# Transposing token rows and score maxima as 64-row products instead of full-array ones in a transformer block on one core

## Chip, core and metric

The kernel runs on one core of one Trainium2 chip. The metric is the device time of one execution in microseconds (us). Before the change it was 718.34 us, the median of three runs (718.19, 718.34 and 720.58). About 0.5%, 3.6 us, is what a measurement of this kernel can tell from no change.

## What is computed

A PixArt block over 16 sequences of 256 tokens and 256 channels: self-attention on a modulated layer norm, cross-attention to a context of 256 tokens, and an MLP of width 1024. Attention has 16 heads of 16 channels.

```python
x_norm = modulate(_ln(x), shift_a, scale_a)
q, k, v = split(x_norm @ W_qkv + b_qkv)                 # 16 heads of 16
x = x + gate_a * (softmax(q k^T * hd**-0.5) v @ W_proj + b_proj)
q_c = _ln(x) @ W_qc + b_qc
k_c, v_c = split(_ln(context) @ W_kvc + b_kvc)
x = x + softmax(q_c k_c^T * hd**-0.5) v_c @ W_cproj + b_cproj
h = gelu(modulate(_ln(x), shift_m, scale_m) @ W_mlp1 + b_mlp1)
x = x + gate_m * (h @ W_mlp2 + b_mlp2)
```

## The kernel before

**Units and beats.** There are 32 attention units: a self unit ("s") and a cross unit ("c") for each of the 16 sequences. The order is five s units, then s and c by turns, and c units at the end. The main loop (`for n in range(-1, nu)`, L1268) gives every unit eight beats, `beat(n, k)` with k from 0 to 7 (L1103). In a beat the tensor engine works on several units at once: raw scores of unit n+1 for its row maxima (`s_tile`, L697, PSUM tile `s`), transposed scores of unit n (`t_part`, L741, PSUM tile `st`), values of unit n or n-1, and projections of units n+2, n+3 and n-2. PE, ScalarE (ACT) and the other engines each issue in the order in which the code is written, so what stands first in `beat` runs first on its engine.

**The pieces of a beat on PE.** `visit` (L1079) issues four products into `s` and four into `st`; between the two it can call `between()`. Behind them `exps` lets ACT read the whole tile `st` through the exponential into a tile `pt`. `st` has one buffer, so nothing can be written into it until that exponential has read it. In the odd beats 24 projection products follow, in the even beats 16 value products (`av_part`, L771), written `o<-pt,v` in the profile. These use 32 columns of the array each and are float32.

**Lanes.** Projections have 64 rows: `lane` (L451) yields the 12 products of one projection on one half of the rows, and `lanes` (L471) pairs two of them, one on rows 0 to 63 and one on rows 64 to 127. A pair runs side by side; it is called a step below. `s` and `st` products (63 and 64 rows) run in such pairs too. `run` (L478) issues a number of steps.

**Transpositions.** A source (normed tokens `xn`, 2 x 128 tokens by 256 channels) is turned by four full-array products against `ident` into a PSUM tile `psT` (`turn` in `transposed`, L377). ACT then rounds it into the high part `xTh`, and DVE or GpSimd makes the rest, `xTl`. Each unit's source T[0] is turned in beat 0 (two products) and beat 2 (two) of the unit three before it; the second source of a c unit, T[1], is turned in beat 4 (four). The row maxima `mx` that DVE takes from `s` are turned by one product for half a unit's heads (`m_turn`, L728), in beat 0 and beat 4. ACT negates the result into `m` (`m_row`, L735), and a transfer writes it into row 63 of the query stack. The product of the maxima goes to a short-lived PSUM tile `psm`, into `psT` (beat 0, with a source) or into `st` (beat 4, with T[1]).

**PSUM.** `ps_gen` (L67) hands out three buffers of the tag "tr" (SHORT: `psT`, `psm`, `o`, q and k projections) and one of the tag "gen" (LONG: v and output projections).

Of the kernel before, what the change touches and what calls it, by code (L numbers as in the profile page):

```python
# [16 lines left out]
P = 128  # L17
# [4 lines left out]
def pixart_block(  # L22
# [29 lines left out]
                return tc.keep_in_program_order(i) if self.on else i  # L52
            return issue

    E_ = {'M': ((-46, -37, -26, -24, -20, -20, -18), (-26, -17, -10, -8, 1, 1, 1), (-3, 1, 4, 7, 9, 9, 9), (8, 11, 13, 15)), 'LN': {'s': 'pool', 'c': 'pool', 'q': 'pool'}, 'ON': (1, 1, 1), 'H': (7, 11, 14, 15), 'AP': 23, 'DV': (1, 2), 'E': (-14, -6, -2, 2), 'HP': (1, 0, 2), 'W1P': [(-9, 3), (-8, 3), (-7, 3), (-6, 3), (-4, 5), (-4, 7), (-3, 1), (-3, 5)], 'W2P': [(-4, 3), (-4, 7), (-3, 2), (-3, 4), (-3, 6), (-3, 7), (-2, 0), (-2, 2), (-2, 4), (-2, 6), (-1, 0)], 'PRE': 'z0qp z0kp load ld2 ld3 rest L0a L0b silu b9 brow turn b2 L0f scale hik lok T0t shift b1 T0h T0l hiq one0a loq hiv bk K0a K0m L1a L1n lov L2a L2b bq K0h K0x K0y L1e K0l K0s Q0a Q0m Q0h Q0x0 Q0y0a T1t Q0l Q0s0 Q0r ldm T1h V0a V0b z1qa T1l bv L2c z1kp L3a L3b L3p L3c K1a K1b', 'SL': {(-1, 0): 'Q1a Q1b K1x K1y K1l K1s', (-1, 1): 'T2t T2h T2p V1a Q1x Q1y Q1l Q1s', (-1, 2): 'V1b rest', (-1, 3): 'rest z2ka', (-1, 4): 'M0 rest one1 ld4', (-1, 5): 'K2a vone', (-1, 6): 'K2m z2qa', (-1, 7): 'cpm2 c1 one2', (0, 0): 'cpm0 rest', (0, 1): 'rest', (0, 4): 'rest', (1, 0): 'rest', (1, 2): 'rest', (1, 4): 'rest'}}
# [321 lines left out]
    def transposed(src, name, scale=None, pool=False):  # L377

        o = Box()

        def place():
            o.ps = ps_gen(f"psT_{name}", SHORT)

        def turn(fs=range(KC)):
            if len(fs) == KC:
                place()
            for f in fs:
                for t in range(NT):
                    PE.transpose(o.ps[:, f * N + t * P:f * N + (t + 1) * P],
                                 src()[:, t, f * P:(f + 1) * P], ident)  # L390

        def high():
# [78 lines left out]
    def lanes(x, y):  # L471


        if x:
            x.ps, x.fresh = ps_gen(f"ps_{x.name}", LONG if x.tok else SHORT), True
        return zip_longest(*(lane(o, half) for half, o in enumerate((x, y)) if o))

    def run(steps, n=12):  # L478
        for _ in islice(steps, n):
# [248 lines left out]
    def m_turn(u, hf, pst=None):  # L728
# [3 lines left out]
        PE.transpose(pst[:16, :P], u.mx[:, hf].rearrange("p r a t -> p (r a t)"), ident)  # L732
        return pst

    def m_row(u, hf, pst):  # L735

        m = work.tile([16, P], F32R, tag="m", name=f"m_{u.n}_{hf}", bufs=1)
        ACT.mul(m, pst[:16, :P], -1.0)
        SP.dma_start(u.q[63:P:64, 4 * hf:4 * hf + 4, :].bitcast(F32), m.bitcast(F32))

    def t_part(u, pair, par):  # L741
# [26 lines left out]
            for f in pieces:  # L768
                next(f)

    def av_part(u, g):  # L771
# [8 lines left out]
        if g == 3:  # L780
            o_out(u, 1)

    def o_out(u, half):
# [295 lines left out]
    def visit(n, k, home=sp, between=None):  # L1079
# [13 lines left out]
        in_turn(*t)  # L1093
        later.append(lambda: exp(units[n], k))

    def spare(n, gate=True):
        p1, _, p3 = (v and v.post for v in map(unit, (n - 1, n - 2, n - 3)))
        if p3 and not p3.added:
# [4 lines left out]
    def beat(n, k):  # L1103
# [25 lines left out]
        kp = None  # L1129
        if k == 5 and lx and n:  # L1130
            kp = lanes(q3.K, None if alone else p2)
        visit(n, k, between=kp and (lambda: run(kp, 2)))
        if k == 0:
            exps()
            if prev:
                av_part(prev, 3)
            if q3 and q3.ready:
                q3.T[0].place()
                pst = m_turn(cur, 1, q3.T[0].ps[:, N:])
                q3.T[0].turn((0,))  # L1140
            else:
                pst = m_turn(cur, 1)
            if prev:
                p1.pull_sums(1)
            m_row(cur, 1, pst)
            if q2:
                q2.K.low()
                q2.K.send_low()
# [3 lines left out]
                p2.low()  # L1152
        elif k == 1:
            exps()
            run(lanes(q2 and q2.Q, q2 and n and q2.V))
            if prev:
                p1.pull_values(1)
            if lc:
# [6 lines left out]
        elif k == 2:  # L1165
            exps()
            if cur:
                av_part(cur, 0)
            if q3:
                q3.T[0].turn((1,) if q3.ready else (0, 1))  # L1170
            if ls:
                ls.ln[0].steps[0]()
            elif prev:
# [24 lines left out]
        elif k == 4:  # L1198
# [2 lines left out]
                p2.end()  # L1201
            if cur:
                av_part(cur, 1)
            if lx:
                lx.T[1].turn()
            if nxt:
                m_part(nxt, 0, st[:, 0] if lx else None)
            if q2:
                q2.Q.low()
                q2.Q.send_low()  # L1210
# [7 lines left out]
                ls.ready = True  # L1218
        elif k == 5:
            exps()  # L1220
            run(kp or lanes(q3 and q3.K, (None if alone else p2) if n else q2.V))
            if cur:
                o_out(cur, 0)
            if lc:
# [8 lines left out]
        elif k == 6:  # L1233
# [139 lines left out]
```

## Time and profile before

| what | number |
|---|---|
| median of three runs | 718.34 us |
| the profiled execution, first to last instruction | 719.7 us |
| granted TensorE clock, mean | 0.999 |
| stage 45 to 490 us (attention): PE busy | 443.51 of 445.00 us |
| the same stage: DVE, ACT, POOL busy | 380.12, 369.82, 335.86 us |
| stage 540 to 719 us (MLP): PE busy | 174.71 of 179.00 us |

A timeline row gives the start in us, the length in us, the engine, operation, output<-inputs, and how many instructions were merged into the row. Product rows overlap, because the recorded length of one product (0.27 to 0.28 us) holds its way through the array; what a product costs is read from one start to the next.

### The profile page before, as it was taken

The page shows a single profiled execution, that of the slowest core. Times are in us where ns is not written, and L with a number is a line of the kernel's source. Part 1 is how long each engine was busy: PE and PEld are TensorE (multiplying, and loading weights), DVE is VectorE, ACT ScalarE, POOL GpSimd, SP SyncE. Part 2 cuts the span into 40 slices and gives each one's busy share as a digit, 9 for nine tenths or more (in the row PEclk, how much of TensorE's full clock was granted, in tenths as well). Part 3 has the DMA queues.
Part 4 walks back from the last instruction along what each step waited for, and adds up shares of the span by engine and source line. Part 5 has one row for each costly group of instructions (what it writes and reads, how often), then busy time and mean ns, then how long its engine had stood idle before and what let it go on. Part 6 is the DMA issues. An engine that isn't in the chain of part 4 may idle for free.

```text
span 719.7 us, 22488 instructions
## 1 busy us (share of the span) xinstructions
PE 710.4 (99%) x8993; PEld 592.3 (82%) x8993; DVE 567.8 (79%) x895; ACT 551.7 (77%) x955; POOL 520.6 (72%) x518
## 2 busy tenths in 40 slices
PE   9999999999999999999999999999999999999997
PEld 8777777777877778777787777777779999999997
DVE  5878888888888798888888888888675777777653
ACT  5677888888888788887888888887867677666661
POOL 7655778787776867776686798977857988656651
PEclk9999999999999999999999999999999999999999
DMA  7574455554545456454655656456323132313212
GB/s 236 183 233 157 160 170 178 175 179 160 167 151 196 162 176 191 163 166 153 195 167 176 210 174 195 156 192 196 95 78 103 59 87 61 88 46 88 66 39 74
DMA packets 81548, 106.15 MB, mean 147 GB/s; under 512 B 16610, under 2 KB 44548, under 8 KB 81444
## 3 DMA queue, kind: packets, MB, share of 16 engines
q1 hardware_dynamic: 80548, 104.37, 45.5%
q8 instruction: 71, 1.16, 0.7%
q10 hardware_dynamic: 896, 0.35, 0.2%
q14 instruction: 33, 0.27, 0.1%
HBM read 35.89 MB, written 8.98 MB: 62 GB/s over the span
## 4 chain that ended last, share of the span: by engine, by line
PE 94%; DVE 3%; POOL 2%; issue 0%; ACT 0%; POOLq 0%; ACTq 0%
PE s L51 18%; PE o L51 16%; PE st L51 16%; PE ph L51 12%; PE ps_qc L51 4%; PE ps_kc L51 4%; PE ps_k L51 4%; PE ps_q L51 3%; PE ps_v_c L51 3%; PE ps_v_s L51 3%; PE ps_P_s L51 2%; DVE mx L51 2%; PE ps_P_c L51 2%; PE psT_c L51 2%; PE psT_s L51 2%; PE psT_q L51 1%
## 5 line engine op out<-in xcount | busy, mean ns | idle before, releaser
L51 DVE TENSOR_REDUCE mx<-s 128x4 f32<-128x1024 f32 x252 | 307.9, 1222 | 73.5 <-PE s L51 70.1
L51 ACT ACTIVATE pt<-st 128x1024 f32<-128x1024 f32 x256 | 263.4, 1029 | 51.8 <-PE st L51 51.0
L51 PE MATMUL o<-pt,v 128*32 128x256 f32 x2048 | 137.1, 385 | 0.0
L51 PE MATMUL s<-big 63*128 63x256 f32 x1008 | 116.8, 305 | 1.7 <-DVE st_q L51 0.8
L51 PE MATMUL st<-big 64*128 64x256 f32 (+1 forms) x1040 | 107.7, 282 | 0.8 <-issue 0.4
L51 PE MATMUL ph<-xTh_m,wself 128*128 128x256 f32 x512 | 100.2, 281 | 0.0
L51 POOL TENSOR_TENSOR hl<-hf,hh 128x512 fp32r<-128x512 f32 x60 | 80.1, 1350 | 20.8 <-ACT hh L51 20.8
L51 PEld LDWEIGHTS s<-big 63*128 63x128 f32 x1008 | 77.3, 185 | 21.0 <-issue 7.1
L51 PEld LDWEIGHTS o<-pt,v 128*32 128x32 f32 x2048 | 53.4, 109 | 39.5 <-ACT oT L51 1.3
L51 PEld LDWEIGHTS st<-big 64*128 64x128 f32 (+1 forms) x1040 | 81.2, 186 | 3.6 <-ACT pt L51 1.5
L51 PEld LDWEIGHTS ph<-xTh_m,wself 128*128 128x128 f32 x512 | 82.3, 188 | 1.2 <-issue 0.4
L51 PE MATMUL ph<-xTl_m,wself 128*128 128x256 f32 x256 | 71.1, 278 | 0.0
L51 ACT ACTIVATE hf<-ph,bT 128x256 f32<-128x256 f32 x112 | 47.0, 473 | 22.1 <-PE ph L51 21.9
L51 ACT ACTIVATE hh<-ph,bT 128x256 fp32r<-128x256 f32 x112 | 47.0, 472 | 19.8 <-PE st L51 8.4
L51 PEld LDWEIGHTS ph<-xTl_m,wself 128*128 128x128 f32 x256 | 48.2, 188 | 0.0
L51 PE MATMUL s<-big,hh 128*128 128x256 f32 x256 | 45.6, 278 | 0.0
L51 DVE TENSOR_SCALAR xn_m<-x,mv_m,rs_m 128x256 f32<-128x256 f32 x28 | 33.5, 1237 | 14.8 <-POOL rs_m L51 14.8
L51 POOL TENSOR_SCALAR xn_q<-x,mv_q,rs_q 128x256 f32<-128x256 f32 x32 | 38.9, 1225 | 1.7
L51 POOL TENSOR_SCALAR xn_c<-c,mv_c,rs_c 128x256 f32<-128x256 f32 x32 | 38.9, 1226 | 1.7
L51 PE MATMUL st<-big,hh 128*128 128x256 f32 x224 | 40.0, 278 | 0.0
L51 PEld LDWEIGHTS s<-big,hh 128*128 128x128 f32 x256 | 38.8, 188 | 0.0
L51 POOL TENSOR_SCALAR rs_c<-mv_c 128x2 f32<-128x2 f32 x16 | 3.6, 228 | 48.3 <-DVE mv_c L51 48.2
(230 smaller groups left out, 2133.1 us busy)
## 6 DMA issues: line engine op xcount, KB each, us to landing
big<-h_k SPq DMA_DIRECT2D x32, 256.0 KB
big<-h_kc SPq DMA_DIRECT2D x32, 256.0 KB
big<-h_qc SPq DMA_DIRECT2D x32, 256.0 KB
big<-h_q SPq DMA_DIRECT2D x30, 256.0 KB
big<-l_k SPq DMA_DIRECT2D x16, 256.0 KB
g<-gd SPq DMA_DIRECT2D x16, 256.0 KB
U_s<-oT SPq DMA_DIRECT2D x32, 128.0 KB
R_s<-rd_s SPq DMA_DIRECT2D x16, 256.0 KB
```

The source lines that it names most:

```text
L51: i = f(*a, **k)
```

## The change

Four things change, and nothing of what is computed.

- `half(h)` turns a source by rows: each of its four products takes 64 rows (tokens 64h to 64h+63 of a tile) and writes 64 columns of `psT`. `turning(T, h, beside)` issues the four between two products of the other lane, in the order t, b, t, t, b, t. The first half is issued at the start of beat 1 (T[0]) or beat 5 (T[1]); the second half in the next beat, between `s` and `st`.
- The maxima are turned by two products of 64 rows and 16 columns (`m_halves`), always into `st`, one in each of its banks. In beat 0 `m` is now sent ahead of the copy `oT` on ACT.
- In beats 1 and 5 one step (with a source to turn) or two steps (without) of the projections are issued between `s` and `st` (`'BT': (1, 2)`). Before, only beat 5 of a c source did so, with two steps.
- In beat 6 the one step behind the value products is left out where T[1] is turned.

```diff
+        def half(h):
+            rows = slice(64 * h, 64 * h + 64)
+            for f in range(KC):
+                for t in range(NT):
+                    c = f * N + t * P + 64 * h
+                    PE.transpose(o.ps[:, c:c + 64], src()[rows, t, f * P:(f + 1) * P], ident[rows, rows])
+                    yield
...
+    def turning(T, h, beside):
+        t = T.half(h)
+        for f in (t, beside, t, t, beside, t):
+            next(f)
...
+    def m_halves(u, hf):
+        for h in range(2):
+            rows = slice(64 * h, 64 * h + 64)
+            PE.transpose(st[:16, h, :64], u.mx[rows, hf].rearrange("p r a t -> p (r a t)"), ident[rows, rows])
+        m_send(u, hf, st[:16, :, :64], lambda m: m.rearrange("p (h q) -> p h q", h=2))
...
+        if k in (1, 5):
+            x, y, T = ((q2 and q2.Q, q2 and n and q2.V, q3 and q3.ready and q3.T[0]) if k == 1 else
+                       (q3 and q3.K, (None if alone else p2) if n else q2.V, lx and lx.T[1]))
+            if T:
+                T.place()
...
+            a, b = pair_of(x, y)
+            steps = weave(a, b)
+            if T:
+                turning(T, 0, b)
+                held.append((T, a))
+            between = lambda: run(steps, E_['BT'][0] if T else E_['BT'][1])
+        elif held:
+            between = lambda: turning(held[0][0], 1, held.pop()[1])
...
         if k == 0:
             exps()
             if prev:
-                av_part(prev, 3)
-            if q3 and q3.ready:
-                q3.T[0].place()
-                pst = m_turn(cur, 1, q3.T[0].ps[:, N:])
-                q3.T[0].turn((0,))
-            else:
-                pst = m_turn(cur, 1)
+                av_part(prev, 3, False)
+            m_halves(cur, 1)
             if prev:
+                o_out(prev, 1)
                 p1.pull_sums(1)
-            m_row(cur, 1, pst)
...
-            if lx:
-                lx.T[1].turn()
             if nxt:
-                m_part(nxt, 0, st[:, 0] if lx else None)
+                m_halves(nxt, 0)
...
-                run(q3.vk, 1)
+                run(q3.vk, 0 if lx else 1)
```

**Beat 0 on PE** (end of the value products, then the start of beat 1), before. `mx` are the maxima, `xn_s` the source, `ps_qc` and `ps_v_c` the two lanes:

```order
L51 MATMUL o_2_2907<-pt_7_2932,v_82 32x256
L51 MATMUL psT_s_2983<-ident,mx_2646 16x128
L51 MATMUL psT_s_2983<-ident,xn_s_2844 128x128 x2
L51 MATMUL s<-big_77 128x256 x4
L51 MATMUL st<-big_80 128x256 x4
```

The same place now:

```order
L51 MATMUL o_2_2957<-pt_7_2980,v_82 32x256
L51 MATMUL st<-ident,mx_2686 16x64 x2
L51 MATMUL psT_s_3048<-ident,xn_s_2885 128x64
L51 MATMUL ps_v_c_2970<-wvch,xTh_c_2807 128x256
L51 MATMUL psT_s_3048<-ident,xn_s_2885 128x64 x2
L51 MATMUL ps_v_c_2970<-wvcl,xTh_c_2807 128x256
L51 MATMUL psT_s_3048<-ident,xn_s_2885 128x64
L51 MATMUL s<-big_77 128x256 x4
L51 MATMUL ps_qc_3049<-xTh_q_2952,wqch 128x256
L51 MATMUL ps_v_c_2970<-wvch,xTh_c_2807 128x256
L51 MATMUL st<-big_80 128x256 x4
```

The maxima's products have moved from `psT` to `st`, and two full products have become four of half the rows, with two lane products among them.

**Beat 4 on PE with a second source** (`xn_q`), before:

```order
L51 MATMUL o_0_2739<-pt_3_2765,v_82 32x256
L51 MATMUL psT_q_2821<-ident,xn_q_2724 128x128 x4
L51 MATMUL st<-ident,mx_2646 16x128
L51 MATMUL s<-big_80 128x256 x4
L51 MATMUL ps_kc_2847<-xTh_c_2762,wkch 128x256
L51 MATMUL ps_P_s_2769<-wself,xTh_as_2677 128x256
```

The same place now:

```order
L51 MATMUL o_0_2786<-pt_3_2810,v_82 32x256
L51 MATMUL st<-ident,mx_2686 16x64 x2
L51 MATMUL psT_q_2888<-ident,xn_q_2765 128x64
L51 MATMUL ps_P_s_2814<-wself,xTh_as_2715 128x256
L51 MATMUL psT_q_2888<-ident,xn_q_2765 128x64 x2
L51 MATMUL ps_P_s_2814<-wself,xTh_as_2715 128x256
L51 MATMUL psT_q_2888<-ident,xn_q_2765 128x64
L51 MATMUL s<-big_80 128x256 x4
```

The four source products no longer stand between the values and the product of the maxima; the maxima come right behind the values.

**The second half, in beat 6 on PE**, now (before, `s` and `st` stood next to each other):

```order
L51 MATMUL s<-big_80 128x256 x4
L51 MATMUL psT_q_2888<-ident,xn_q_2765 128x64
L51 MATMUL ps_kc_2889<-xTl_c_2808,wkch 128x256
L51 MATMUL psT_q_2888<-ident,xn_q_2765 128x64 x2
L51 MATMUL ps_kc_2889<-xTl_c_2808,wkch 128x256
L51 MATMUL psT_q_2888<-ident,xn_q_2765 128x64
L51 MATMUL st<-big_78 128x256 x4
```

Two products of the lane whose projection was held back run among the four.

More of the change, by code (lines that the diff above doesn't have):

```diff
@@ L390, in turn @@
                                  src()[:, t, f * P:(f + 1) * P], ident)
+        def half(h):
[5 more added lines that the diff above has]
+                    yield
+        o.half = half
         def high():
@@ L475, in lanes, with pair_of, weave @@
             x.ps, x.fresh = ps_gen(f"ps_{x.name}", LONG if x.tok else SHORT), True
-        return zip_longest(*(lane(o, half) for half, o in enumerate((x, y)) if o))
+        return weave(*pair_of(x, y))
+    def pair_of(x, y):
+        return [lane(o, half) if o else iter(()) for half, o in enumerate((x, y))]
+    def weave(*gens):
+        return zip_longest(*gens)
+    def turning(T, h, beside):
+        t = T.half(h)
+        for f in (t, beside, t, t, beside, t):
+            next(f)
     def run(steps, n=12):
@@ L733, in m_turn, with m_send @@
         return pst
+    def m_halves(u, hf):
[3 more added lines that the diff above has]
+        m_send(u, hf, st[:16, :, :64], lambda m: m.rearrange("p (h q) -> p h q", h=2))
     def m_row(u, hf, pst):
+        m_send(u, hf, pst[:16, :P], lambda m: m)
+    def m_send(u, hf, src, form):
         m = work.tile([16, P], F32R, tag="m", name=f"m_{u.n}_{hf}", bufs=1)
-        ACT.mul(m, pst[:16, :P], -1.0)
+        ACT.mul(form(m), src, -1.0)
         SP.dma_start(u.q[63:P:64, 4 * hf:4 * hf + 4, :].bitcast(F32), m.bitcast(F32))
@@ L769, in in_turn, with av_part @@
                 next(f)
-    def av_part(u, g):
+    def av_part(u, g, out=True):
         if g % 2 == 0:
@@ L779, in av_part @@
                           start=(c == 0), stop=(c == NT - 1), tile_position=(0, h * 32))
-        if g == 3:
+        if g == 3 and out:
             o_out(u, 1)
@@ L1094, in visit @@
         later.append(lambda: exp(units[n], k))
+    held = []
     def spare(n, gate=True):
@@ L1128, in beat, with rest_of @@
                 p2.end()
[L1129 to L1132, printed above, removed]
+        between = None
+        if k in (1, 5):
[3 more added lines that the diff above has]
+                T.place()
+            if x:
+                x.ps, x.fresh = ps_gen(f"ps_{x.name}", LONG if x.tok else SHORT), True
+            a, b = pair_of(x, y)
[6 more added lines that the diff above has]
+            between = lambda: turning(held[0][0], 1, held.pop()[1])
+        visit(n, k, between=between)
+        def rest_of():
+            run(steps, 10 - E_['BT'][0] if held else 12)
         if k == 0:
@@ L1154, in beat @@
             exps()
-            run(lanes(q2 and q2.Q, q2 and n and q2.V))
+            rest_of()
             if prev:
@@ L1168, in beat @@
                 av_part(cur, 0)
-            if q3:
-                q3.T[0].turn((1,) if q3.ready else (0, 1))
+            if q3 and not q3.ready:
+                q3.T[0].turn()
             if ls:
@@ L1220, in beat @@
             exps()
-            run(kp or lanes(q3 and q3.K, (None if alone else p2) if n else q2.V))
+            rest_of()
             if cur:
```

2 lines of the change are left out of this document (1 added, 1 removed).

## The prediction

> **What bounds the kernel now.** I read the page first, then the PE timeline of one unit, then ACT beside it. All times are in us.
>
> ```profile
> PE 710.4 (99%) x8993; PEld 592.3 (82%) x8993; DVE 567.8 (79%) x895; ACT 551.7 (77%) x955; POOL 520.6 (72%) x518
> ```
>
> PE is busy from end to end. What it issues, and any wait put into it, adds to the time directly; the other engines have a fifth of the span free. So the sum is made on PE, from start to start. One unit, beats 0 to 4, whose source is the context of a c unit:
>
> ```profile
> 205.29 1.07 PE L51 MATMUL o<-pt,v 128*32 128x256 f32 x16
> 206.29 0.28 PE L51 MATMUL psT_c<-ident,mx 128*16 128x128 f32 x1
> 206.41 0.38 PE L51 MATMUL psT_c<-ident,xn_c 128*128 128x128 f32 x2
> 206.72 0.51 PE L51 MATMUL s<-big 63*128 63x256 f32 x4
> 207.06 0.40 PE L51 MATMUL st<-big 64*128 64x256 f32 x4
> 207.30 0.31 PE L51 MATMUL ps_v_s<-wself,xTh_s 64*128 64x256 f32 x1
> ...
> 208.71 0.44 PE L51 MATMUL s<-big 63*128 63x256 f32 x4
> 208.95 0.43 PE L51 MATMUL st<-big 64*128 64x256 f32 x4
> ...
> 210.31 0.44 PE L51 MATMUL psT_c<-ident,xn_c 128*128 128x128 f32 x2
> 210.68 0.51 PE L51 MATMUL s<-big 63*128 63x256 f32 x4
> 211.03 0.41 PE L51 MATMUL st<-big 64*128 64x256 f32 x4
> ...
> 214.21 0.66 PE L51 MATMUL psT_q<-ident,xn_q 128*128 128x128 f32 x4
> 214.75 0.28 PE L51 MATMUL st<-ident,mx 128*16 128x128 f32 x1
> 214.95 0.51 PE L51 MATMUL s<-big 63*128 63x256 f32 x4
> 215.30 0.28 PE L51 MATMUL ps_P_s<-wself,xTh_as 64*128 64x256 f32 x1
> ```
>
> Prices to be seen here. A full-array transposition is 0.11 (two last 0.38, one of them 0.27). From the maxima's product to `s` is 0.20: 0.11 of the product and about 0.09 to change the array's division. Four `s` products are 0.24 behind lane products (208.71 to 208.95), but 0.35 behind a full-array or 32-column product (214.95 to 215.30). A lane step is 0.117: 12 steps from 207.30 to 208.71. From the end of the values to `st` it takes 0.77 in beat 0 and 0.72 in beat 2; in beat 4 it takes 1.09 until the lane step that is issued ahead of `st`.
>
> ACT in the same beats:
>
> ```profile
> 205.59 1.02 ACT L51 ACTIVATE pt<-st 128x1024 f32<-128x1024 f32 x1
> 206.50 0.60 ACT L51 COPY oT<-o 128x512 f32<-128x512 f32 x1
> 206.96 0.26 ACT L51 ACTIVATE m<-psT_c 16x128 fp32r<-16x128 f32 x1
> 207.50 1.03 ACT L51 ACTIVATE pt<-st 128x1024 f32<-128x1024 f32 x1 [0.28 <-PE st L51]
> ...
> 213.65 1.05 ACT L51 ACTIVATE pt<-st 128x1024 f32<-128x1024 f32 x1
> 215.06 0.27 ACT L51 ACTIVATE m<-st 16x128 fp32r<-16x128 f32 x1 [0.37 <-PE st L51]
> ```
>
> The exponential is still reading `st` when the value products are through: in beat 0 it ends at 206.61, 0.32 after they make room at 206.29; in beat 4 at 214.70, 0.49 after 214.21. In beat 4 the maxima already go into `st` today: they start at 214.75, 0.05 after the exponential's end. Four source products stand ahead of them and fill that time. These two gaps decide the case.
>
> How often each occurs, by the tile into which the maxima are turned (count behind the x):
>
> ```profile
> L51 PE MATMUL psm<-ident,mx 128*16 128x128 f32 x20 | 5.5, 277 | 0.0
> L51 PE MATMUL psT_c<-ident,mx 128*16 128x128 f32 x16 | 4.4, 277 | 0.0
> L51 PE MATMUL st<-ident,mx 128*16 128x128 f32 x16 | 4.4, 276 | 0.0
> L51 PE MATMUL psT_s<-ident,mx 128*16 128x128 f32 x12 | 3.3, 277 | 0.0
> ```
>
> Beat 0 with a source: 16 + 12 = 28 units. Beat 4 with a second source: 16. Of the 20 `psm`, two belong to the start; 15 are beats 4 without a second source and 3 beats 0 at the end.
>
> **The price of a 64-row product.** None is in the trace. It loads 128 columns, as a full one does, and streams 64. The nearest from below is a transposition of 16 rows that loads 128 columns and streams 16 (first row); from above, the full one:
>
> ```profile
> 5.21 0.20 PEld L51 LDWEIGHTS st<-ident,c_sb 16*128 16x128 f32 x2
> ```
>
> ```profile
> 206.29 0.09 PEld L51 LDWEIGHTS psT_c<-ident,mx 128*16 128x16 f32 x1 [0.41 <-issue]
> 206.30 0.25 PEld L51 LDWEIGHTS psT_c<-ident,xn_c 128*128 128x128 f32 x2
> ```
>
> Two loads of the first kind last 0.20, two of the second 0.25, one 0.14 in both: they follow each other at 0.06 and 0.11. The second spacing is that of the 128 streamed columns, since the load behind it is fetched while they stream (at 206.41, when the product of the row above starts). Half the columns are 0.055, hidden by a 0.06 load. I take 0.062, near the lower row; the ends are 0.055 and 0.11. A turning is then 4 x 0.062 = 0.25, beside two lane products of 0.23; at the upper end 0.44.
>
> The Trainium skill, page "TensorE: Matmul & The Clock Gate", section "Part 3: Packing small matmuls — row/col tiling", speaks against the change: a weight load overlaps running products only when it goes to another row group. By that rule the four products in one lane would be load plus stream each; the full-array rows above, at 0.11 with the load fetched under the stream, do not bear it out.
>
> **The change part by part.**
>
> Beat 0, 28 times. The maxima wait for the exponential, 0.32 + 0.05 = 0.37, because everything behind them on PE's queue (source, `s`, lanes) waits too. Two products of 64 columns side by side are 0.055, and the change of division behind them 0.10 (as built they take 32 columns of the array, the lanes 128, so it stays): 0.155. The turning costs 0.25, and 0.11 for the slow start behind a change; then `s` 0.24. That is 0.37 + 0.155 + 0.36 + 0.24 = 1.125, less the lane step half done inside (two of a lane's twelve products, 0.117) = 1.01. Before: 0.77. **+0.24 x 28 = +6.7.** Bounds for the wait: nothing, if the exponential ended in time, and 0.49 as in beat 4.
>
> Beat 0 without a source, 3 times, and beat 4 without a second one, 15 times. For these a self unit's beat 4:
>
> ```profile
> 230.10 0.28 PE L51 MATMUL psm<-ident,mx 128*16 128x128 f32 x1
> 230.31 0.51 PE L51 MATMUL s<-big 63*128 63x256 f32 x4
> 230.66 0.40 PE L51 MATMUL st<-big 64*128 64x256 f32 x4
> ```
>
> ```profile
> 229.47 1.02 ACT L51 ACTIVATE pt<-st 128x1024 f32<-128x1024 f32 x1
> ```
>
> 0.56 before. Now the exponential's end, 230.49, is 0.39 behind 230.10: 0.44 + 0.155 + 0.35 = 0.945, **+0.385 x 15 = +5.8**; in beat 0 with 0.37: 0.875, **+0.315 x 3 = +0.9**.
>
> Beat 4 with a second source, 16 times: 0.54 + 0.155 + 0.36 + 0.24 - 0.117 = 1.18 against 1.09, and its second half in beat 6 another 0.25 - 0.117 = 0.13: **+0.22 x 16 = +3.5.**
>
> Beat 2, 28 times: no source products behind the values, so `s` follows at once, 0.35 in place of 0.72; the second half costs 0.13: **-0.24 x 28 = -6.6.** Here `s` needs DVE to have read its predecessor:
>
> ```profile
> 209.18 1.22 DVE L51 TENSOR_REDUCE mx<-s 128x4 f32<-128x1024 f32 x1 [0.54 <-PE s L51]
> ```
>
> It ends at 210.40; with the turning ahead of `st`, `s` would come at 210.31 + 0.25 = 210.56, so this cover of 0.16 holds. Without it beat 2 would give 0.16 of its 0.24 back.
>
> Beat 6 of a c source, the step left out behind the values:
>
> ```profile
> 218.53 0.38 PE L51 MATMUL ps_kc<-xTh_c,wkch 64*128 64x256 f32 x1
> 218.75 0.40 PE L51 MATMUL s<-big 63*128 63x256 f32 x4
> ```
>
> Step and `s` are 0.22 + 0.24 today; now `s` 0.35 and the step 0.117 later. Nothing. The steps moved between `s` and `st` are the same work in another place: nothing on PE. They cover the new wait of `st` for `m`: `m` starts 0.31 after its product and takes 0.27, done some 0.63 with the signal, while turning, `s` and step need 0.155 + 0.36 + 0.24 + 0.117 = 0.87, or, without a source, 0.155 + 0.35 + 0.23 = 0.74. On ACT `oT` moves behind `m`: in beat 0 it would end at 206.61 + 0.05 + 0.31 + 0.27 + 0.60 = 207.84, and the next exponential follows `st` by 0.44 (207.06 to 207.50) at 206.29 + 1.13 + 0.12 + 0.44 = 207.98. Hidden, by 0.14. DMA is the same transfer of `m` from SP's queue, half a microsecond later and four beats before its reader.
>
> **Sum.** 6.7 + 0.9 + 5.8 + 3.5 - 6.6 = +10.3. The MLP stage is untouched. The profiled execution, 719.7, becomes 730.0; it lies 1.4 above the median, and 718.34 + 10.3 = **728.6 us, slower by 1.4%.** The terms rest on waits and prices that I trust to some 0.1 in 62 to 88 places, 6 to 9 in all, so by itself this case lies between 722 and 737.
>
> **The rivals.**
>
> *The maxima do not wait (faster).* If the exponentials of beats 0 and 4 ended before the value products, 28 x 0.37 + 3 x 0.37 + 16 x 0.54 + 15 x 0.44 = 26.7 would fall out: 718.3 + 10.3 - 26.7 = 702. It breaks even when the 62 maxima wait 0.17 less each. For it: ACT is idle 23% of the span. Against it: in both units shown the exponential ends 0.32 to 0.49 late, and nothing in the change moves it forward. Chance 0.14.
>
> *The 64-row products do not pack (slower still).* If load and stream of one lane add, 0.062 + 0.055 = 0.117 each, a turning is 0.47 instead of 0.25; there are 2 x 28 + 2 x 16 = 88: +19, 748. The same place decides whether the change does what it says: a turning that does not run beside the other lane costs 0.25 + 0.23, the same 748. For it: no row shows such a mixture. Against it: lane steps show two loads and two products side by side. Chance 0.14. It is what the page's rule above would give.
>
> *Gains and waits cancel.* If a change of division cost twice the 0.09 read here where a full product stood, beats 0, 2 and 4 would gain 0.1 more at 28 + 28 + 16 places, 7 in all: 721. For it: `s` is slow behind both kinds of product. Against it: the rows give the same 0.35 behind either. Chance 0.10.
>
> **How the numbers follow.** The forecast has 0.62, all of it slower by over 0.5% (3.6 us, about what a measurement of this kernel can tell from no change); with the second rival slower is 0.76, same 0.10, faster 0.14. The range holds the forecast's own 722 to 737, the cancelling case, and half of the other two: 712 to 744.
>
> **What would show it.** Right: in the profile after, `st<-ident,mx` starts 0.05 behind the end of an exponential in beats 0 and 4, and PE's idle time ended by ACT `pt` grows from almost nothing to some 20 us; 64-row products follow each other at about 0.06 in a lane; `s` follows the values directly in beat 2. Wrong: maxima that start as soon as the values are through; a turning longer than 0.3; `s` in beat 2 held by DVE; or `st` held by `m`.

## The result and the profile after

| | median of the runs | ratio to before, 95% |
|---|---|---|
| before, in the same job | 719.06 us (4 runs) | |
| after the change | 737.34 us (737.21 to 737.52, 4 runs) | 1.0252 (1.0237 to 1.0267) |

The change makes the kernel slower by 18.3 us. The forecast was 728.6, slower by 10.3; 737.3 lies inside its range of 712 to 744, but above the 722 to 737 of its own case.

First the page of after, the busy time of each engine (the row beside the first one of the prediction):

```profile
span 735.6 us, 22982 instructions
PE 703.8 (96%) x9232; PEld 589.8 (80%) x9232; DVE 568.1 (77%) x895; ACT 556.8 (76%) x955; POOL 521.3 (71%) x518
```

PE was busy for 710.4 of 719.7 us; now it is 703.8 of 735.6. PE is busy for less time than before and idle for 31.8 us in place of 9.3. So this is a matter of waits. The view of what PE waited for (total, times, longest) names one:

```profile
PE st L51 <- ACT pt L51: 25.1, 65, 1.1
```

Before, the same row was `PE st L51 <- ACT pt L51: 0.4, 2, 0.2`. The groups of instructions (busy time and mean ns of one, then the idle time before them) show which product waits:

```profile
L51 PE MATMUL st<-ident,mx 64*16 64x64 f32 x126 | 14.1, 221 | 24.7 <-ACT pt L51 24.7
L51 PE MATMUL psT_q<-ident,xn_q 64*128 64x64 f32 x128 | 13.4, 224 | 0.0
```

The products of the maxima take 24.7 of these 25.1 us; the source's 64-row products wait for nothing. One unit of after, from the value products of beat 0 to the turning of beat 2, on PE:

```profile
245.92 1.07 PE L51 MATMUL o<-pt,v 128*32 128x256 f32 x16
247.38 0.22 PE L51 MATMUL st<-ident,mx 64*16 64x64 f32 x2 [0.38 <-ACT pt L51]
247.41 0.36 PE L51 MATMUL ps_v_s<-wself,xTh_s 64*128 64x256 f32 x1
247.44 0.35 PE L51 MATMUL psT_c<-ident,xn_c 64*128 64x64 f32 x3
247.62 0.27 PE L51 MATMUL ps_v_s<-wself,xTh_s 64*128 64x256 f32 x1
247.62 0.23 PE L51 MATMUL psT_c<-ident,xn_c 64*128 64x64 f32 x1
247.66 0.48 PE L51 MATMUL s<-big 63*128 63x256 f32 x4
...
249.47 0.51 PE L51 MATMUL s<-big 63*128 63x256 f32 x4
...
249.82 0.28 PE L51 MATMUL psT_c<-ident,xn_c 64*128 64x64 f32 x2
```

and what ACT and DVE do beside it:

```profile
246.30 1.02 ACT L51 ACTIVATE pt<-st 128x1024 f32<-128x1024 f32 x1
247.69 0.27 ACT L51 ACTIVATE m<-st 16x128 fp32r<-16x128 f32 x1 [0.37 <-ACT pt L51]
```

```profile
248.19 1.23 DVE L51 TENSOR_REDUCE mx<-s 128x4 f32<-128x1024 f32 x1 [0.38 <-PE s L51]
```

Three things are to be read here. The exponential ends at 247.32 and the maxima start 0.06 later, though the values were through at about 246.92: the wait that was forecast. The turning takes 0.22 (247.44 to 247.66), with two products of the other lane inside; three of its products are merged into a row of 0.35 whose last one alone would be 0.23, so they stand 0.06 apart: the price that was forecast. And in beat 1, where the turning has taken two lane steps out, the next `s` comes at 249.47, 0.05 behind the end of DVE's reduction of the `s` before (248.19 + 1.23 = 249.42). That one was not forecast.

To see where the time goes I took the mean length of each beat, from the first `s` product to the next beat's, out of the trace. The rows are units with a source in beat 0 and a second one in beat 4 (16 units), and units with a source in beat 0 only (12):

```
beat                         0     1     2     3     4     5     6     7
16 units   before         2.06  2.00  1.97  1.96  2.31  1.97  1.83  1.80
           after          2.34  1.82  1.97  1.96  2.46  1.82  1.97  1.98
12 units   before         2.09  2.00  1.95  1.95  1.82  1.97  1.84  1.89
           after          2.38  1.81  1.97  1.96  2.08  2.09  1.82  1.83
```

Summed with their counts: +3.3 us in beats 0 to 3 of these 28 units, +5.2 in beats 4 to 7 of the 16 and +3.6 in those of the 12. Ahead of these units it is +4.2, and behind them -0.4. Together that is 15.9, the difference of the two profiled executions (735.6 - 719.7). The medians differ by 2.4 more: a run's time here is 1.8 above its span (737.38 for 735.6), so the profiled execution of before is one of some 721.5, 2.4 above the median of 719.06.

The start is the place where after's longest wait stands, 1.12 us ahead of the first unit's maxima. The view by windows (us, each engine's busy time and count in the order PE, PEld, DVE, ACT, POOL, then the granted clock, the DMA share and GB/s), for after:

```profile
35.00:40.00 5.00, 5.00 (x43) 4.24 (x46) 2.83 (x4) 1.95 (x2) 0.51 (x1) 0.62 0.65 228
40.00:45.00 5.00, 5.00 (x56) 3.78 (x52) 2.69 (x6) 2.43 (x6) 0.00 (x0) 0.70 0.33 95
```

The same two windows before:

```profile
35.00:40.00 5.00, 5.00 (x64) 4.03 (x65) 4.03 (x6) 3.44 (x5) 0.93 (x1) 1.00 0.59 209
40.00:45.00 5.00, 5.00 (x81) 3.97 (x80) 4.40 (x10) 4.30 (x8) 1.60 (x3) 1.00 0.60 200
```

The clock is 1.00 there. PE is "busy" all the time in both kernels here, but after it gets through 43 and 56 products in place of 64 and 81.

### The profile page after: what moved, and what is told of

Its sections match the earlier page's. It is cut to its first block, busy times and chain, and to the rows that moved or that the text cites. A ratio compares the mean times of both kernels' runs of the same rounds, so it can differ in the third digit from the quotient of the medians.

```text
span 735.6 us, 22982 instructions
## 1 busy us (share of the span) xinstructions
PE 703.8 (96%) x9232; PEld 589.8 (80%) x9232; DVE 568.1 (77%) x895; ACT 556.8 (76%) x955; POOL 521.3 (71%) x518
## 5 line engine op out<-in xcount | busy, mean ns | idle before, releaser
L51 DVE TENSOR_REDUCE mx<-s 128x4 f32<-128x1024 f32 x252 | 308.1, 1223 | 89.7 <-PE s L51 84.3
L51 ACT ACTIVATE pt<-st 128x1024 f32<-128x1024 f32 x256 | 263.3, 1029 | 63.9 <-PE st L51 60.4
L51 PE MATMUL o<-pt,v 128*32 128x256 f32 x2048 | 137.9, 387 | 0.0
L51 PE MATMUL s<-big 63*128 63x256 f32 x1008 | 121.4, 309 | 0.6
L51 PE MATMUL st<-big 64*128 64x256 f32 (+1 forms) x1040 | 114.8, 290 | 0.6 <-ACT pt L51 0.4
L51 PEld LDWEIGHTS s<-big 63*128 63x128 f32 x1008 | 79.3, 187 | 28.3 <-DVE mx L51 22.2
L51 PE MATMUL ph<-xTh_m,wself 128*128 128x256 f32 x512 | 99.6, 280 | 0.0
L51 POOL TENSOR_TENSOR hl<-hf,hh 128x512 fp32r<-128x512 f32 x60 | 80.5, 1359 | 20.0 <-ACT hh L51 20.0
L51 PEld LDWEIGHTS st<-big 64*128 64x128 f32 (+1 forms) x1040 | 84.9, 187 | 5.7 <-ACT pt L51 1.5
L51 PEld LDWEIGHTS o<-pt,v 128*32 128x32 f32 x2048 | 53.6, 109 | 39.6 <-issue 0.7
L51 PEld LDWEIGHTS ph<-xTh_m,wself 128*128 128x128 f32 x512 | 81.9, 188 | 1.2 <-issue 0.4
L51 PE MATMUL ph<-xTl_m,wself 128*128 128x256 f32 x256 | 70.9, 277 | 0.0
L51 ACT ACTIVATE hf<-ph,bT 128x256 f32<-128x256 f32 x112 | 47.3, 476 | 20.8 <-PE ph L51 20.6
L51 ACT ACTIVATE hh<-ph,bT 128x256 fp32r<-128x256 f32 x112 | 47.2, 475 | 18.4 <-PE st L51 8.9
L51 PEld LDWEIGHTS st<-ident,mx 64*16 64x16 f32 x126 | 5.5, 84 | 54.7 <-ACT pt L51 54.7
L51 PEld LDWEIGHTS ph<-xTl_m,wself 128*128 128x128 f32 x256 | 48.2, 188 | 0.0
L51 PE MATMUL s<-big,hh 128*128 128x256 f32 x256 | 45.2, 277 | 0.0
L51 DVE TENSOR_SCALAR xn_m<-x,mv_m,rs_m 128x256 f32<-128x256 f32 x28 | 33.5, 1235 | 14.8 <-POOL rs_m L51 14.8
L51 POOL TENSOR_SCALAR rs_c<-mv_c 128x2 f32<-128x2 f32 x16 | 3.7, 230 | 58.2 <-DVE mv_c L51 58.0
L51 PE MATMUL ps_P_s<-wself,xTh_as 64*128 64x256 f32 x256 | 41.0, 281 | 0.0
L51 POOL TENSOR_SCALAR xn_c<-c,mv_c,rs_c 128x256 f32<-128x256 f32 x32 | 39.0, 1229 | 1.7
L51 POOL TENSOR_SCALAR xn_q<-x,mv_q,rs_q 128x256 f32<-128x256 f32 x32 | 39.0, 1229 | 1.7
```

Source lines behind the costliest of these rows:

```text
L51: i = f(*a, **k)
```

## The experiments

Theories: **the waits** of the maxima for the exponential are the loss; **the turning** is the loss; **DVE's reduction** holds the beats that the turning shortens; **the start** costs by its clock. Times below are medians, and differences are to the runs of before in the same job (after: +18.3).

### e1: the exponentials in two halves

```diff
-        for h in range(2):
-            rows = slice(64 * h, 64 * h + 64)
-            PE.transpose(st[:16, h, :64], u.mx[rows, hf].rearrange("p r a t -> p (r a t)"), ident[rows, rows])
-        m_send(u, hf, st[:16, :, :64], lambda m: m.rearrange("p (h q) -> p h q", h=2))
+        m_part(u, hf, st[:, 0])
...
+        if pair % 4 == 0:
+            for r in range(2):
+                ACT.activation(u.pt[pair][:, r].rearrange("p c n -> p (c n)"), st[:, r], AF.Exp, scale=SCALE)
```

> The change, with the exponentials of pairs 0 and 4 (those that still read st when the maxima of beats 0 and 4 come) cut into two instructions, one for each half of st, and the maxima turned by one full 128-row product into the first half, so that they wait for the first half of the exponential alone. If the waits of the maxima for the exponential are what costs (some 0.4 us at 62 places, about 20 us in the profile after), they vanish and the time falls by 18 to 22 us, to 715 to 720; the PE idle time ended by ACT pt falls from 25 us to below 8. If that idle time is covered anyway by what limits the beats (VectorE's reduction in beats 1 and 5), the time falls by less than 6 us.

Measured: 747.79 us, +27.3, ratio 1.0383 (1.0359 to 1.0407). Neither theory expected a loss. PE's and ACT's rows show why:

```profile
210.25 0.28 PE L51 MATMUL st<-ident,mx 128*16 128x128 f32 x1 [0.43 <-ACT pt L51]
210.46 0.50 PE L51 MATMUL s<-big 63*128 63x256 f32 x4
```

```profile
209.12 1.08 ACT L51 ACTIVATE pt<-st 128x512 f32<-128x512 f32 x2
```

The two halves end together at 210.20, and the maxima start 0.05 behind the second. In the program as built the two halves share one signal, which stands behind the second; the edit never took the wait away. It did add two prices: the exponential is 0.06 longer (1.08 for 1.02), and from the maxima to `s` it takes 0.48 in the mean with a source and 0.21 without, where the 64-row products of the change took 0.30 to 0.35 and 0.03. That is 0.06 and some 0.15 in 62 places, 13 us; 9 are seen, since beat 5 of the 12 units, among others, gets 0.14 back. So this run says nothing on the theories, but it measures what two narrow products save.

### e2: the maxima of the change without its turning

```diff
-            x, y, T = ((q2 and q2.Q, q2 and n and q2.V, q3 and q3.ready and q3.T[0]) if k == 1 else
-                       (q3 and q3.K, (None if alone else p2) if n else q2.V, lx and lx.T[1]))
+            x, y, T = ((q2 and q2.Q, q2 and n and q2.V, None) if k == 1 else
+                       (q3 and q3.K, (None if alone else p2) if n else q2.V, None))
...
+                q3.T[0].place()
+                q3.T[0].turn((0,))
...
+                lx.T[1].turn()
```

> The change's maxima (two 64-row products into st, in beats 0 and 4), with the sources turned by full-array products at their old places, so without the turning in the lanes. If the waits of the maxima are the cost, the time stays above before by about the whole difference or more: 736 to 742. If the turning in the lanes is the cost (64-row products that do not run beside the other lane), the time falls to 722 to 728.

The steps between `s` and `st` and the order of `m` and `oT` stay as changed here, and the step of beat 6 is back. Measured: 743.97, +23.5, ratio 1.0330 (1.0303 to 1.0357), 2 us above what the theory of the waits allowed and far from that of the turning. The moved maxima without the turning cost more than the whole change, and the turning in the lanes gives some 5 us back. Beat 0 grows by 0.48 and 0.45 us here, more than in after, since the source's two full products again follow the wait: from the maxima to `s` it takes 0.52 in the mean. The moved steps are not the loss: beat 1, which has two of them, is 0.03 shorter than before. In beat 4 of units with a second source the four source products cover the wait, as they did before: the beat is 0.10 shorter than before, and beat 5 0.16 longer.

### e3: the first unit's maxima as before

```diff
-            m_halves(cur, 1)
+            if n:
+                m_halves(cur, 1)
+            else:
+                m_part(cur, 1)
```

> The change, with the maxima of beat 0 of the first unit alone turned as before (full-array product into psm, no wait for the exponential). In the profile after this one wait is 1.1 us, and TensorE's granted clock then stands at 0.5 from 36.2 to 43.0 us. If the clock falls because of that wait, the time falls by 4 to 5 us, to 732 to 733.5, and the clock stays at 1.0 there; if the fall of the clock has another cause, only the wait itself is gained, 1.2 us, and the clock still falls.

Measured: 732.96, +12.4, ratio 1.0188 (1.0165 to 1.0211), as expected of the wait. This one wait of 1.12 us, once in the program, is worth about 4.5 us: the stretch ahead of unit 1 is 4.3 us shorter than in after. The same two windows:

```profile
35.00:40.00 5.00, 5.00 (x70) 4.04 (x69) 4.03 (x6) 3.56 (x5) 0.83 (x1) 1.00 0.59 211
40.00:45.00 5.00, 4.63 (x77) 3.54 (x78) 4.20 (x9) 3.84 (x7) 2.10 (x3) 1.00 0.60 177
```

### e4 and e7: a shorter reduction, in the change and before

```diff
-            DVE.tensor_reduce(mx[:, :, g // 2, a, t], home.rearrange("p r (j n) -> p r j n", j=2),
+            DVE.tensor_reduce(mx[:, :, g // 2, a, t], home.rearrange("p r (j n) -> p r j n", j=2)[:, :, :, :N // 2],
```

The second half of the keys is left out of the maxima.

> The change, with VectorE's reductions over the first half of the keys alone: the second half of the keys is left out of the maxima, so a reduction takes about 0.7 in place of 1.23 us. If the steps that a turning takes out of beats 1 and 5 are not gained there because the next s waits for VectorE's reduction of the s before, the time falls by about 0.19 us for each of the 44 turnings, 8 us or more, to 726 to 730. If VectorE is not in the way, the time changes by less than 2 us.

> The kernel before, with VectorE's reductions over the first half of the keys alone: the second half of the keys is left out of the maxima. The control to the same edit of the change, which gained 6.5 us. If VectorE's reduction holds only beats that the turning has shortened, before gains less than 2.5 us: 716 to 719. If a shorter reduction helps any beat, it gains about the same 6.5 us: 711 to 713.

Measured: 730.79 for the change, ratio 1.0148 (1.0133 to 1.0164), so about 1.0% less than the change has; 714.70 for before, ratio 0.9931 (0.9910 to 0.9952), 0.7% less. The first is just above its 726 to 730, the second lies between its two forecasts, and the totals do not tell the two apart. The beats do: in the change beats 1, 2, 5 and 6 of units with two sources shorten by 0.08, 0.08, 0.09 and 0.08, and beats 0, 3, 4 and 7 by nothing; in before those four beats shorten by 0.00 to 0.03, and the gain is spread over beats 0 and 7 of the 12 units and the rest of the program. So DVE's hold is real in the change, 0.16 to 0.17 for each turning or some 7 us in all, but part of what the totals show has nothing to do with it. One hold shows in two beats: `s` starts later, and behind that wait, in beat 2, its four products take 0.34 until the next product, where they take 0.24 in e4. e9 and e11 bear on that.

### e5 and e6: the maxima into a bank of their own

```diff
-            m_halves(cur, 1)
+            m_part(cur, 1)
...
-                m_halves(nxt, 0)
+                m_part(nxt, 0)
```

The first line alone is e5, both are e6.

> The change, with the maxima of beat 0 turned by one full-array product into a bank of their own (psm), as beats 0 without a source did before; the sources stay in the lanes and beat 4 stays as changed. If the waits of the maxima for the exponential are the cost, beat 0 loses its wait of 0.37 us less 0.10 us that the full product costs more, at 31 places, and the first unit's 4.5 us go too: 13 us less than the change, 722 to 727. If the turning ahead of s is the cost, only the first unit's 4.5 us go: 732 to 734.

> The change, with the maxima of beats 0 and 4 both turned by one full-array product into psm: the half of the change that moves the maxima into st is undone, the half that moves the sources into the lanes is kept. If the waits are the whole cost, beat 4 gains 0.3 us at 15 and 0.4 us at 16 places on top of the run with beat 0 alone, and the kernel is faster than before: 706 to 713. If a bank for psm does not come free in time, or if VectorE's reduction holds the beats at 1.80 us, the gain of beat 4 is lost: 718 to 724.

Measured: 741.77, +22.4, ratio 1.0304 (1.0282 to 1.0325), and 739.17, +19.8, ratio 1.0282 (1.0259 to 1.0305). Both misses, though neither has the loss of the start (the clock is 1.00 in both windows). The waits of e6:

```profile
PE psT_c L51 <- ACT m L51: 7.2, 14, 0.8
PE psT_q L51 <- ACT m L51: 6.9, 15, 0.6
PE psT_s L51 <- ACT m L51: 5.5, 11, 0.5
```

The wait for `pt` is gone and one for `m` stands in its place, 19.6 us in 40 places. In the program as built `psm` and the `psT` behind it are given the same one of the three SHORT banks, and the first source product has to wait until ACT has read the maxima. Before, the source's second half came two beats later, and the maxima lay in columns that only it overwrites.

### e8 and e9: no wait for the exponential, none for m

```diff
+    def m_beside(u, hf, T, free):
+        T.place()
+        src = T.ps[:16, N:].rearrange("p (t h q) -> p t h q", t=2, h=2)[:, :, free]
+        PE.transpose(src, u.mx[:, hf].rearrange("p r a t -> p (r a t)"), ident)
+        rows.append(lambda: m_send(u, hf, src, lambda m: m.rearrange("p (h q) -> p h q", h=2)))
...
-                turning(T, 0, b)
-                held.append((T, a))
+                turning(T, 1, a)
+                held.append((T, 0, b))
+                rows.pop()()
```

Since the lane beside the second half now ends an accumulation there, ACT's copies of `v` and of the output projection (beats 2 and 6) stand behind `visit` in place of ahead of it. Without a source the maxima go into a bank of their own by one full product, as before the change, and no step stands between `s` and `st`.

> The sources stay in the lanes; the maxima go by one full-array product into columns of the source's own bank that the first half does not write (the bank of beat 0 before), and are read only behind that half, so that they wait neither for the exponential nor, as in the two runs with psm, the source for the maxima's reader. Rows 64 to 127 of a source are turned first, since the other order lacks a wait between two products of one bank. If the moved waits are what made the change slow, and the turning in the lanes itself pays, beats 0 to 2 take 0.26 us less than before at 28 units and beats 4 to 6 0.42 less at 16: 14 us less than before, 701 to 709. If VectorE's hold of 1.80 us on beats 1 and 5 or the slow start behind each turning eats the gain, it stays within 4 us of before: 715 to 722.

> The same with VectorE's reductions over the first half of the keys alone: the second half of the keys is left out of the maxima. If VectorE holds the beats that the turning shortens, the time falls by a further 6 to 10 us, above what the same edit gave before (4.6 us), and beats 1, 2, 5 and 6 of units with a source shorten by 0.08 each, as in the change; if not, it falls by no more than 4.6.

Measured: 754.89, +34.8, ratio 1.0483 (1.0443 to 1.0523), the slowest kernel of all and far outside both expectations; and with the half reduction 718.81, ratio 0.9984 (0.9966 to 1.0001). 36 us between the two, where the same edit gave before 4.6. PE's rows of e8, and DVE's:

```profile
219.98 0.27 PE L51 MATMUL psT_c<-ident,xn_c 64*128 64x64 f32 x1
220.70 0.38 PE L51 MATMUL ps_q<-xTh_s,wself 64*128 64x256 f32 x1 [0.45 <-DVE l_k L51]
220.71 0.40 PE L51 MATMUL psT_c<-ident,xn_c 64*128 64x64 f32 x3
220.91 0.36 PE L51 MATMUL s<-big 63*128 63x256 f32 x1
```

```profile
218.64 1.23 DVE L51 TENSOR_REDUCE mx<-s 128x4 f32<-128x1024 f32 x1 [0.85 <-PE s L51]
219.78 0.87 DVE L51 SCALAR_TENSOR_TENSOR l_k<-ps_k,bqkv,h_k 128x256 fp32r<-128x256 f32 x2
```

With rows 64 to 127 turned first, the lane beside them is the one that begins a new accumulation (`ps_q`), and it waits until DVE has made `l_k` out of an older tile, at 220.65. DVE gets to `l_k` behind the reduction. So the turning, and `s` behind it, wait for DVE once more, by another tile; the view of waits has 20 us of this in 44 places. With the half reduction `l_k` is early enough and the wait is gone: beats 0 and 4 account for 21 of the 36 us. Beats 1, 2, 5 and 6 of the 16 units shorten by 0.12, 0.07, 0.12 and 0.07, and beats 1 and 2 of the 12 by 0.13 and 0.07: the hold of the change once more, some 8.5 us. So DVE it is, in two places, and the half reduction merely brings e8 back to the time of before. What the turning stands ahead of decides: in this form it delays `s`, and with it DVE.

### e10 and e11: the turning behind st

The same maxima beside the source, but each first half stands behind `st`, beside the lane that ends an older accumulation, as in the change; `m` is sent behind it. Without a source the maxima go as in e8, and no step stands between `s` and `st` in any beat.

```diff
         def rest_of():
+            if T:
+                turning(T, 0, b)
+                held.append((T, 1, a))
+                rows.pop()()
-            run(steps, 10 - E_['BT'][0] if held else 12)
+            run(steps, 10 if T else 12)
```

> As in the run without the new wait (maxima into free columns of the source's own bank), but each turning's first half stands behind st in beats 1 and 5, beside the lane that finishes an older accumulation (as in the change), and the second half between s and st of the beat after. So s follows the maxima directly, no lane step waits for VectorE to clear its bank, and VectorE gets its s earlier. If only waits and the hold of VectorE made the turning in the lanes a loss, a unit takes 0.22 less than before in beat 0, 0.12 less in beat 2 (28 units), 0.54 less in beat 4 and 0.13 more in beat 6 (16 units): 16 us less than before in all, and with a third of it eaten by ScalarE or VectorE still 10: 702 to 709. If the turning costs by itself what it saves, 716 to 721.

> The run with the turning behind st, with VectorE's reductions over the first half of the keys alone: the second half of the keys is left out of the maxima. There s of beats 1 and 5 comes early, and no beat is shorter than 1.79 us in the mean; if VectorE's reduction held the turning's beats only because the change shortened them to that reduction's length, the gain is now that of the kernel before, 4.6 us, or less: 702 to 706. If VectorE limits these beats in any order, it is 8 us or more: below 699.

Measured: 706.62, -13.4, ratio 0.9821 (0.9791 to 0.9850), inside the expected 702 to 709 and faster than both kernels; with the half reduction 704.72, ratio 0.9785 (0.9756 to 0.9813), which is no more than the 4.6 that before gained. The page of e10, its wait for the exponential, and PE in beats 0 and 1:

```profile
PE 698.1 (99%) x9169; PEld 588.2 (83%) x9169; DVE 563.3 (80%) x895; ACT 551.1 (78%) x955; POOL 520.6 (74%) x518
```

```profile
PE st L51 <- ACT pt L51: 0.4, 2, 0.2
```

```profile
202.25 1.07 PE L51 MATMUL o<-pt,v 128*32 128x256 f32 x16
203.25 0.28 PE L51 MATMUL psT_c<-ident,mx 128*16 128x128 f32 x1
203.46 0.51 PE L51 MATMUL s<-big 63*128 63x256 f32 x4
203.81 0.41 PE L51 MATMUL st<-big 64*128 64x256 f32 x4
204.05 0.22 PE L51 MATMUL psT_c<-ident,xn_c 64*128 64x64 f32 x1
204.06 0.28 PE L51 MATMUL ps_v_s<-wself,xTh_s 64*128 64x256 f32 x1
204.10 0.28 PE L51 MATMUL psT_c<-ident,xn_c 64*128 64x64 f32 x2
204.17 0.28 PE L51 MATMUL ps_v_s<-wself,xTh_s 64*128 64x256 f32 x1
204.23 0.22 PE L51 MATMUL psT_c<-ident,xn_c 64*128 64x64 f32 x1
```

From the end of the values to `s` it takes 0.21, where before took 0.43; the turning takes 0.21 (204.05 to 204.26) with two lane products inside. The mean beats:

```
beat                         0     1     2     3     4     5     6     7
16 units   e10            1.84  2.00  1.87  1.96  1.80  2.03  1.91  1.96
12 units   e10            1.79  2.00  1.87  2.03  1.83  1.97  1.83  1.80
```

Beat 0 gains 0.22 and 0.30, beat 2 gains 0.10 and 0.08 and beat 4 of the 16 units gains 0.51, nearly what was expected; beats 5 to 7 of the 16 units give 0.30 back in place of 0.13. The beats with a first half in them, 1 and 5, are 2.00 and 2.03 long, well above what a reduction asks for, and a half reduction now gains 1.9 us in all.

### e12: e1 with a signal of its own

```diff
+        pst = m_turn(u, hf, st[:, 0])
+        second.pop()()
+        m_row(u, hf, pst)
```

`second` holds the second half of the exponential, so the product stands between the halves.

> The run with the exponentials of pairs 0 and 4 in two halves once more, with the maxima's product written between the two halves, so that the built program has the first half signal by itself (in the first try the two halves shared one signal behind the second). If the waits of the maxima for the exponential are a cost that PE pays in full, each of 62 places loses 0.38 us and pays 0.10 for the full product: 17 us less than the change, 718 to 723, with at most 8 us left of the 25 us that PE waited for pt; st of the next beat may then wait for m, which takes some of it back, up to 728. If they are covered, no more than 5 us less: above 732.

Measured: 728.74, +8.4, ratio 1.0106 (1.0080 to 1.0133): some 10 us less than the change, 0.7 above the upper end of what the first theory allowed. The waits of PE:

```profile
PE st L51 <- ACT m L51: 2.6, 12, 0.4
PE st L51 <- ACT pt L51: 1.0, 3, 0.7
```

25.1 us of waits for `pt` are down to 1.0, and beats 0 and 4 are 0.24 to 0.32 shorter than in the change: 15.6 us in all. Beats 2, and beats 6 of the 16 units, are 0.09 shorter too, 4 us. But beats 1 and 5 are 0.18 to 0.28 longer again, 12 us. The rows of ACT show one reason:

```profile
217.76 0.62 ACT L51 ACTIVATE pt<-st 128x512 f32<-128x512 f32 x1
218.74 0.60 ACT L51 ACTIVATE pt<-st 128x512 f32<-128x512 f32 x1 [0.37 <-PE st L51]
219.24 0.25 ACT L51 ACTIVATE m<-st 16x128 fp32r<-16x128 f32 x1
```

The second half now waits for the maxima's product, though it reads other columns of `st`, so it ends at 219.34, `m` at 219.49, and `st` of the next beat starts at 219.54. The wait has moved one tile on. The start kept 0.69 us of its wait.

## Why the prediction was right, and where it was not

The direction and the mechanism were right: the maxima wait for an exponential that is still reading `st`. What was forecast as 0.37, 0.54 and 0.44 us at 62 places and some 20 us in all measured 24.7 with the start's 1.12, about 0.38 each, as idle time of PE; read from start to start, as the forecast was, the means are 0.43, 0.51 and 0.44. e2 shows the moved maxima as a loss without the turning, e10 that the turning without these waits is a gain of 13 us. By the terms of the sum:

- **Beat 0 with a source, "+6.7", and beat 2, "-6.6"**: together 0.1, measured +3.3 over beats 0 to 3. The wait was right. From the maxima to `s` the forecast has 0.155 for the maxima and 0.36 for the turning with a slow start, 0.515 in all; 0.30 and 0.34 were measured (means of the 16 and the 12 units). The first source product follows the maxima after 0.06 in 12 of the 28 units and after 0.10 in the others, and the turning has no slow start. What failed is the gain of beat 2. The sentence on DVE ("this cover of 0.16 holds") set the reduction of beat 2's `s` against the `s` behind beat 2, and there it does hold. The `s` that DVE holds is the one before, behind the shortened beat: beat 1 lost two lane steps, 0.23, and cannot be shorter than the reduction allows. By the rows above that is 0.53 from `s` to the reduction (247.66 to 248.19), 1.23 for it and 0.05 to the next `s`: 1.81, and 1.82 and 1.81 were measured. e4 shows the hold as 0.16 for a turning in beats 1 and 2, or 4.7 us over these 28 units. Without it the two terms would have come out at -1.4, better than forecast.
- **Beat 4 with a second source, "+3.5"**: measured +5.2. Beats 5 and 6 have the same hold, 0.17 together, 2.7 us; without it 2.5 are left, less than forecast. The step left out of beat 6, "Nothing" in the forecast, was indeed nothing: it only moves time from beat 6 to beat 7, which is 0.18 longer. In e4, without the hold, beat 6 is 0.05 and beat 7 0.20 longer than before, together the 0.25 of the second half. In one of the 16 units `st` of beat 7 waited for the exponential of beat 6, 0.52 behind `s`; in the other 15 it stands 0.34 to 0.35 behind it.
- **Beat 4 without a second source, "+5.8"** for 15 units: +3.6 measured for 12 of them, 0.30 each in place of 0.385: 0.26 in beat 4 for the cheaper maxima, with 0.03 to `s`, and 0.12 in beat 5, less 0.08 in beats 6 and 7. In beat 5 `st` did wait for `m`, which I had called covered: in all 12 units it starts 0.05 behind the end of `m`. The cheaper maxima had taken away part of that cover.
- **The start**: not in the sum at all. Two of the `psm` products "belong to the start" and were left there. Moving one of them into `st` cost one wait of 1.12 us and then, with clocks of 0.62 and 0.70 in two windows of 5 us, 5 x 0.38 + 5 x 0.30 = 3.4 us: together the 4.5 of e3.
- **The price of a 64-row product**, 0.062, was right (0.06), so the rival in which load and stream of one lane add falls. The Trainium skill, page "TensorE: Matmul & The Clock Gate", section "Part 3: Packing small matmuls — row/col tiling", lets a load overlap running products only for another row group; the rows of after and of e10 do not agree, at 0.06 for products of one row group that follow each other.

Between the two profiled executions the miss is 5.6 us (15.9 for 10.3): the start (+4.2) and DVE's hold (+7.3), less some 3.4 by which the other prices in these 28 units came out lower, and 2.5 in the last units (forecast +2.1, measured -0.4). That errors of both signs met here is luck; without it the time would have lain still further above the forecast's own 722 to 737. The hold is the step that failed most: it was looked for behind beat 2 and lay one beat earlier. The forecast also set the span of 719.7 against the median of the run times ("1.4 above the median"); a run of that span takes some 721.5, 3.2 above it. That did not enter the forecast.

## What to carry to other kernels

Cutting work out of a stage gains only down to the next engine's period: before a beat is shortened, write down for each engine what the shortest beat is, and check that at the beat that gets shorter and at the one behind it. A tile into which a small result is moved brings the reader of that tile onto the critical queue, and PSUM buffers that several tiles share do the same with a name that the edit never mentions; e5, e8 and e12 each took away one such wait and met the next. What helped in e10 was to keep the maxima out of `st`, to let `s` follow them directly and to put the turning behind `st`.

## What the runs showed of the hardware that I had not expected

- The granted clock fell to 0.62 and 0.70 in the two windows behind one wait of 1.12 us at the start. In e12 0.69 us were enough for one window; PE's row and the window:

```profile
33.53 0.28 PE L51 MATMUL st<-ident,mx 128*16 128x128 f32 x1 [0.69 <-ACT pt L51]
```

```profile
35.00:40.00 5.00, 5.00 (x45) 3.57 (x42) 3.11 (x4) 2.05 (x2) 0.52 (x1) 0.66 0.58 200
```

  It fell there in e1, e2 and e4 too, whose first unit waits 1.12 to 1.18 us, and not in e3, which has all the other waits of the change. The Trainium skill, page "TensorE: Matmul & The Clock Gate", section "Part 1: The HAM clock gate (the "warmup" mystery)", speaks of an idle window of about 3.4 us; here a wait a third to a fifth as long was followed by the fall. In e1 and e12 the maxima's product is a full one, so the 64-row products of the change are not needed for the fall. Whether the wait alone decides, or the sparse work around it too, was not tried.
- Two products of the maxima with 64 rows each and 16 columns, side by side, hold up a 64-row source product behind them by 0.06 or 0.10 and `s` by 0.03 (means of after), where the full product of the same maxima holds up either by 0.21 (e1).
- A row of waits of weight loads (PEld) need not be a cost: `PEld s L51 <- DVE mx L51: 24.1, 57, 1.0` stands in e10, which gains 0.3% from a shorter reduction; after has `PEld s L51 <- DVE mx L51: 22.2, 52, 0.6` and gains 1.0%.
